# The head of a GRU kernel: the order of its weight loads, of its bias products and of the first turn of x

## The chip, the cores and the metric

The kernel runs on one core of a Trainium2 chip. The core has a matrix engine (TensorE, PE in the profile), a vector engine (VectorE, DVE), an activation engine (ScalarE, ACT), a general engine (GpSimd, POOL) and a queue engine (SyncE, SP). Transfers between DRAM and the core's memory are issued by SP, ACT or POOL and carried by 16 DMA engines. The metric is the device time of one execution in microseconds (us), the median of three runs.

## The reference, cut to what matters

A GRU runs over 256 time steps, and its states go through an expert-choice layer; x is added to the result.

```
x: [16, 256, 512]   W_ih, W_hh: [512, 1536]   b_ih, b_hh: [1536]   h0: [16, 512]
for t in 0..255:
    gi = x[:, t] @ W_ih + b_ih ;  gh = h @ W_hh + b_hh        # three gates of 512 columns: r, z, n
    r = sigmoid(gi_r + gh_r) ;  z = sigmoid(gi_z + gh_z)
    n = tanh(gi_n + r * gh_n)
    h = (1 - z) * n + z * h
y = expert-choice layer over the 4096 states (router softmax, top 256 tokens of each of 16 experts, one 512 x 512 matrix)
out = x + y
```

All of it is in float32. The steps are a chain: step t+1 can't start before h of step t is there.

## The kernel before, in words

The program has three stages: a head, a loop over the 256 steps, and a tail. The change touches the head only (lines 68 to 88, 440 to 474 and 722 to 777).

**Tiling.** Time is cut into 32 groups of 8 steps (TG = 8, NG = 32). A group of x is 128 rows (16 batch rows by 8 steps) of 512 columns, one slice `xs[:, g, :]`. W_ih lies in the tile `wih` in four row blocks k = 0..3, each 128 rows by 1536 columns (768 KB). W_hh lies in `whh`, and is loaded by gate: gate 0 is r, 1 is z, 2 is n, 1024 KB each. The input product of a pair p of steps, x times W_ih, is made by `x_part(p, k, bank, gates)` (line 613): four small matmuls for one row block k, each in its own quarter of the matrix engine. Its left operand is x turned, `xT`, which `spread_x` (line 729) makes: four transposes on TensorE into an idle PSUM bank, then four copies on VectorE, one for each pair of the group.

**Loads before (lines 453 to 474).** ACT's queue takes x's group 0, blocks 0 and 1 of W_ih, gate 0 and three quarters of gate 1 of W_hh. SP's queue takes blocks 2 and 3, x's group 1, gate 2, the last quarter of gate 1 and eight pieces of x's group 2 (`xa`, line 415). A one-element memset on POOL into block 2 (line 457) makes SP's first load wait a little. POOL's queue takes the initial state c0 and, at the end, the three bias rows (line 474).

**Work before (lines 722 to 777).** The order on PE, DVE, ACT and POOL is written out by hand. VectorE makes some masks (`make_masks`, from index rows that POOL writes); TensorE clears six PSUM banks (`begin_sums`, line 90, a bf16 matmul with zeros, 512 columns wide) and runs two more such matmuls to stay busy (`keep_clock`, line 717). Then `spread_x(0)`, two more idle matmuls, and the input product of the pairs 0 to 3 block by block, k = 0, 1, 2, 3. After block 1, c0 is turned (line 748). After block 2 come the bias products (`biases`, line 489: 16 matmuls of one or two rows that spread the biases over 128 rows into `l_bank`), two VectorE operations that copy them out (lines 756 and 757), and `spread_x(1)`. After block 3 come the sums `x_done` on VectorE, and the input products of the pairs 4 and 5, which need all four blocks, then one idle matmul, and step 0 begins (`h_part`, line 697, matmuls at line 705). `mixes` (line 640) are VectorE subtractions of blocks of W_ih for later products; part 0 needs blocks 0 and 1, part 1 needs all. Step 0 multiplies by the gates in the order r, n, r, n, z.

The loop and the tail are the same before and after.

Of the kernel before, what the change touches and what calls it, by code (L numbers as in the profile page):

```python
# [11 lines left out]
I32 = mybir.dt.int32  # L12
AF = mybir.ActivationFunctionType
ALU = mybir.AluOpType
# [3 lines left out]
def kernel(  # L18
# [27 lines left out]
    xs = const.tile([P, NG, D], F32, name="xs")  # L46
# [4 lines left out]
    wih = const.tile([P, KC, 3, D], F32, name="wih")  # L51
# [6 lines left out]
    GH = P // E  # L58
# [7 lines left out]
    ones_b = const.tile([P, B], F32, name="ones_b")  # L66
    zero = xs[:, NG - 1, D - P // 2 :].bitcast(BF16)
    nc.gpsimd.memset(zero, 0.0)
    make_identity(nc, ident)

    def make_masks():

        nc.gpsimd.memset(ones_b, 1.0)
        shift = GH.bit_length() - 1
        at = xs[:, 10, 0:3].bitcast(I32)
        nc.gpsimd.iota(at[:, 0:1], pattern=[[0, 1]], base=0, channel_multiplier=1)
        nc.vector.tensor_single_scalar(at[:, 1:2], at[:, 0:1], shift, ALU.logical_shift_right)
        nc.vector.tensor_single_scalar(at[:, 2:3], at[:, 0:1], GH - 1, ALU.bitwise_and)
        at_f = xs[:, 11, 0:3]
        nc.vector.tensor_copy(at_f, at)  # L80
        to_i = xs[:, 11, P : 3 * P].bitcast(I32).rearrange("p (o e h) -> p o e h", o=2, h=GH)
        nc.gpsimd.iota(to_i[:, 0, :, :], pattern=[[1, E], [0, GH]], base=0, channel_multiplier=0)
        nc.gpsimd.iota(to_i[:, 1, :, :], pattern=[[0, E], [1, GH]], base=0, channel_multiplier=0)
        to = xs[:, 10, P : 3 * P].rearrange("p (o n) -> p o n", o=2)
# [277 lines left out]
    with (  # L362
# [13 lines left out]
        bias = wts.tile([P, 4, P], F32, name="bias")  # L376
# [4 lines left out]
        C2 = 3 * P // 2  # L381
        spare = xs[:, RING:, :].rearrange("p g d -> p (g d)")[:, AHEAD * 3 * P : AHEAD * 3 * P + C2]
# [9 lines left out]
        c0 = xs[0:B, 7, :]  # L392
        ones = wts.tile([2, QD], F32, name="ones")
# [32 lines left out]
        def new_xa():  # L426
            return xap.tile([P, TG // 2, P], F32, name="xa")
# [12 lines left out]
        with tc.manual_schedule(engines={ET.SP, ET.Activation, ET.Pool}):  # L440
            def load_gate(gate, queue, ks=slice(0, KC)):
                queue.dma_start(
                    out=whh[:, ks, gate, :],
                    in_=w_hh[:, gate * D : (gate + 1) * D].rearrange("(c p) n -> p c n", c=KC)[:, ks, :],
                )

            def load_k(k, queue):
                queue.dma_start(
                    out=wih[:, k].rearrange("p g d -> p (g d)"),
                    in_=w_ih.rearrange("(p c) n -> p c n", c=KC)[:, k, :],  # L450
                )

            nc.scalar.dma_start(out=xs[:, 0, :], in_=x[:, 0:TG, :])
            load_k(0, nc.scalar)
            load_k(1, nc.scalar)
            nc.gpsimd.dma_start(out=c0, in_=cond)
            nc.gpsimd.memset(wih[0:1, 2, 0, 0:1], 0.0)
            load_k(2, nc.sync)
            load_k(3, nc.sync)
            nc.sync.dma_start(out=xs[:, 1, :], in_=x[:, TG : 2 * TG, :])  # L460
            load_gate(0, nc.scalar)
            load_gate(2, nc.sync)
            load_gate(1, nc.scalar, slice(0, KC - 1))
            load_gate(1, nc.sync, slice(KC - 1, KC))
            xa_next = new_xa()
            for c in range(KC):
                load_xa(2, xa_next, c, (nc.sync, nc.sync))
            nc.scalar.activation(dummy, ones[0:1, 0:1], AF.Sigmoid)
            for dst, src in (
                (b_raw[0:1], b_ih.rearrange("(o g d) -> o g d", o=1, d=D)),  # L470
                (b_raw[1:2], b_hh.rearrange("(o g d) -> o g d", o=1, d=D)),
                (b_n, b_hh[2 * D :].rearrange("(o d) -> o d", o=1)),
            ):
                nc.gpsimd.dma_start(out=dst, in_=src)

        def load_expert(part, s):

# [11 lines left out]
        def biases(bank):  # L489
            for i, rows in enumerate((b_raw[:, 0, :], b_raw[:, 1, :], b_raw[0:1, 2, :], b_n)):  # L490
                for j in range(KC):
                    nc.tensor.matmul(
                        bank[quadrant(j), P * i : P * (i + 1)],
                        ones[0 : rows.shape[0]],
                        columns(rows, j),
                        start=False,
                        stop=True,
                        tile_position=(0, QD * j),
                        skip_group_check=True,
                    )  # L500
# [216 lines left out]
        def keep_clock(n, banks=idles):  # L717

            for i in range(n):
                begin_sums(banks[i % len(banks)])  # L720

        with tc.manual_schedule(engines={ET.PE, ET.Activation, ET.DVE, ET.Pool}):
            make_masks()
            for bank in banks:
                begin_sums(bank)
            keep_clock(2)
            held = (r_bank, n_bank, z_bank, x_bank0, x_bank1, idles[1])

            def spread_x(g, bank):
                xT[g] = xtp.tile([P, TG // 2, P], F32, name="xt")  # L730
                for c in range(KC):
                    nc.tensor.transpose(bank[:, P * c : P * (c + 1)], xs[:, g, c::KC], ident)
                for q in range(TG // 2):
                    to = xT[g][:, q, :].rearrange("p (c o b) -> p c o b", c=KC, b=B)
                    nc.vector.tensor_copy(
                        to, bank.rearrange("p (c b t) -> p c t b", c=KC, t=TG)[:, :, 2 * q : 2 * q + 2, :]
                    )

            spread_x(0, idles[0])
            keep_clock(2, (idles[1],))  # L740
            for k in range(KC):
                for p in range(KC):
                    for gates in (slice(0, 1), slice(1, 3)) if p == k == 0 else (slice(0, 3),):
                        x_part(p, k, held[p], gates, start=False)
                if k == 1:
                    mixes(0)
                    for c in range(KC):
                        nc.tensor.transpose(
                            idles[0][:, B * c : B * (c + 1)], c0[:, P * c : P * (c + 1)], ident[0:B, 0:B]
                        )  # L750
                    nc.vector.tensor_copy(
                        hs[:, :, 0, :], idles[0][:, 0 : KC * B].rearrange("p (k b) -> p k b", b=B)
                    )
                elif k == 2:
                    biases(l_bank)
                    nc.vector.tensor_copy(bias, l_bank.rearrange("p (g d) -> p g d", d=P))
                    nc.vector.tensor_tensor(spare, bias_f[:, C2 : 2 * C2], bias_f[:, 0:C2], ALU.subtract)
                    spread_x(1, idles[0])
                    x_sums(1)
                elif k == 3:  # L760
                    mixes(1)
            for p in range(KC):
                x_done(p, held[p])
                if p == 0:
                    preset_first(0)
                elif p == 2:
                    preset_rest(0)
            for p in (KC, KC + 1):
                for k in range(KC):
                    for gates in (slice(0, 1), slice(1, 3)):  # L770
                        x_part(p, k, held[p], gates, start=False)
                if p == KC:
                    mixes(3)
                x_done(p, held[p])
# [6 lines left out]
        with tc.manual_schedule(engines={ET.PE, ET.Activation, ET.DVE, ET.Pool, ET.SP}):  # L781
# [6 lines left out]
            for s in range(T):  # L788
                p, odd = divmod(s, 2)
# [476 lines left out]
```

## Time and profile before

| what | us |
|---|---|
| median of three runs | 1114.39 (1114.12 to 1115.35) |
| the profiled execution, its own time | 1114.45 |
| its span in the trace | 1112.6 |
| first matmul of step 0 (line 705) | 25.72 |
| TensorE busy | 1101.7 (99% of the span) |

Times in the profile count from the start of the span. "PEld" is the weight load of TensorE, which runs beside its matmuls. A float32 matmul shows as two records. The end of a matmul is modelled, so that the distance from start to start is what a row of matmuls costs. A DMA's time "to landing" counts from the start of its issue until its semaphore says that all of it has arrived.

### The profile page before, as it was taken

The numbers are of one execution on the slowest core, as the hardware profiler recorded it, in microseconds if no ns is written. First come the engines' busy times: TensorE is split into PE (matmuls) and PEld (weight loads), VectorE is DVE, ScalarE is ACT, GpSimd is POOL, SyncE is SP. The second block draws the span as 40 slices with busy tenths as digits, with TensorE's granted clock in tenths as the row PEclk, the third lists the DMA queues.
The fourth block names the chain that finished last, engine by engine and source line by source line (L and its number), as shares of the span: only waits on it lengthen the run. The fifth ranks groups of instructions, "written<-read, shape, count | busy, mean of one in ns | idle before, by whom it ended". The sixth has DMA issues, their size and how long they took to land.

```text
span 1112.6 us, 77160 instructions
## 1 busy us (share of the span) xinstructions
PE 1101.7 (99%) x34291; PEld 957.8 (86%) x34291; DVE 802.0 (72%) x4664; ACT 579.0 (52%) x2644; POOL 30.0 (3%) x173
## 2 busy tenths in 40 slices
PE   9999999999999999999999999999999999999998
PEld 4888888888888888888888888888888888888763
DVE  4777666776777676767767677777777777777786
ACT  1555555555555555555555555555555555554551
POOL 1000000000000000000000000000000000000000
PEclk9999999999999999999999999999999999999999
DMA  7200000000000000000000000000000000002437
GB/s 258 63 11 12 12 12 14 19 21 21 21 21 12 12 14 14 14 14 12 12 12 12 14 14 14 14 12 12 12 12 14 14 15 14 4 4 80 136 108 238
DMA packets 34371, 37.34 MB, mean 34 GB/s; under 512 B 6112, under 2 KB 23776, under 8 KB 34032
## 3 DMA queue, kind: packets, MB, share of 16 engines
q1 hardware_dynamic: 32544, 28.64, 8.9%
q8 instruction: 270, 4.42, 1.6%
q10 hardware_dynamic: 1360, 3.67, 0.9%
q14 instruction: 69, 0.57, 0.2%
q0 software_dynamic: 128, 0.05, 0.0%
HBM read 23.94 MB, written 8.39 MB: 29 GB/s over the span
## 4 chain that ended last, share of the span: by engine, by line
PE 93%; DVE 4%; ACT 1%; DMA 1%; issue 0%; ACTq 0%; DVEq 0%
PE gates L705 59%; PE x L678 20%; PE gates L678 4%; PE pe L586 3%; PE x L308 3%; PE pe L308 2%; PE pe L115 1%; DVE nT L897 1%; DMA wih<-in_L_cond_W_ih_dram 1%; DVE t L859 1%; DVE zT L900 1%; PE gates L618 1%; ACT r L798 1%; ACT t L863 1%; PE x L618 0%
## 5 line engine op out<-in xcount | busy, mean ns | idle before, releaser
L705 PE MATMUL gates<-whh,hs 128*16 128x128 f32 x24576 | 722.1, 273 | 3.1 <-DVE hs L911 2.4
L705 PEld LDWEIGHTS gates<-whh,hs 128*16 128x16 f32 x24576 | 652.0, 103 | 57.0 <-DVE hs L911 50.5
L798 ACT ACTIVATE r<-gates 128x128 f32<-128x128 f32 x256 | 70.9, 277 | 232.8 <-PE gates L705 232.8
L802 DVE COPY seen<-r 1x1 f32<-1x1 f32 x256 | 36.3, 142 | 199.7 <-ACT r L798 199.4
L900 DVE STREAM_TRANSPOSE zT<-zs 128x32 f32<-128x32 f32 (+1 forms) x768 | 165.7, 216 | 0.0
L863 ACT ACTIVATE t<-t 128x64 f32<-128x64 f32 x512 | 103.1, 248 | 104.2 <-DVE t L861 104.2
L897 DVE STREAM_TRANSPOSE nT<-t 128x64 f32<-128x64 f32 x512 | 100.2, 234 | 48.1 <-ACT t L863 48.1
L908 DVE TENSOR_TENSOR v<-u,zT 128x32 f32<-128x32 f32 x512 | 98.7, 193 | 8.8
L911 DVE TENSOR_TENSOR hs<-v,nT 128x32 f32<-128x32 f32 x512 | 95.4, 186 | 8.7
L678 PE MATMUL x<-wih,xt 128*32 128x192 f32 (+2 forms) x1968 | 101.7, 325 | 0.0
L861 DVE TENSOR_TENSOR t<-t,xs 128x64 f32<-128x64 f32 x512 | 90.8, 220 | 0.0
L678 PE MATMUL x<-wih,xs 128*32 128x192 f32 x1952 | 90.5, 326 | 0.0
L859 DVE TENSOR_TENSOR t<-r,gates 128x64 f32<-128x64 f32 x512 | 90.3, 218 | 0.0
L865 ACT ACTIVATE zs<-gates 128x64 f32<-128x64 f32 x512 | 86.6, 221 | 0.0
L903 DVE TENSOR_TENSOR u<-hs,nT 128x32 f32<-128x32 f32 x512 | 78.3, 153 | 0.0
L678 PEld LDWEIGHTS x<-wih,xt 128*32 128x32 f32 x1968 | 62.4, 110 | 11.8
L678 PEld LDWEIGHTS x<-wih,xs 128*32 128x32 f32 x1952 | 62.2, 110 | 11.9
L511 ACT COPY ht<-hs 128x128 f32<-128x128 f32 (+1 forms) x128 | 52.0, 408 | 0.7 <-DVE hs L911 0.7
L678 PE MATMUL x<-xs 128*32 128x192 f32 (+1 forms) x1040 | 50.9, 316 | 0.0
L678 PE MATMUL x<-xs,xt 128*32 128x192 f32 x976 | 50.8, 326 | 0.0
L678 PE MATMUL gates<-xs 128*32 128x192 f32 x976 | 50.8, 326 | 0.0
L881 ACT COPY x<-x 128x192 f32<-128x192 f32 x61 | 18.5, 303 | 62.0 <-PE x L678 62.0
(199 smaller groups left out, 938.6 us busy)
## 6 DMA issues: line engine op xcount, KB each, us to landing
out_dram<-xs SPq DMA_DIRECT2D x31, 256.0 KB, 3.7
xa<-in_x_dram SPq DMA_DIRECT2D x240, 32.0 KB, 2.9
xs<-in_x_dram SPq DMA_DIRECT2D x27, 256.0 KB, 4.1
wih<-in_L_cond_W_ih_dram ACTq DMA_DIRECT2D x2, 768.0 KB, 6.4
wih<-in_L_cond_W_ih_dram SPq DMA_DIRECT2D x2, 768.0 KB, 9.6
whh<-in_L_cond_W_hh_dram ACTq DMA_DIRECT2D x1, 1024.0 KB, 15.7
whh<-in_L_cond_W_hh_dram SPq DMA_DIRECT2D x1, 1024.0 KB, 17.8
ewr<-in_L_ffn_expert_w_dram SPq DMA_DIRECT2D x4, 256.0 KB, 3.0
```

The lines of the kernel that those rows point to most:

```text
L678: nc.tensor.matmul(dst[quadrant(j), at:to], lhs[:, QD * k : QD * (k + 1)], columns(rows[k], j)[:, at // QD : to // QD], start=False, stop= ...
L705: nc.tensor.matmul(dst[quadrant(j, m)], lhs, columns(whh[:, k, gate_, :], j), start=False, stop=(k == KC - 1), tile_position=(0, QD * j), ...
L798: nc.scalar.activation(r, rr[p % 2], AF.Sigmoid)
L859: nc.vector.tensor_tensor(t[half], r[:, cols], hn[p % 2][:, cols], ALU.mult)
L861: nc.vector.tensor_tensor(t[half], t[half], ring[:, p % AHEAD, 2, cols], ALU.add)
L863: nc.scalar.activation(t[half], t[half], AF.Tanh)
L865: nc.scalar.activation(zs[half], zz[p % 2][:, cols], AF.Sigmoid)
L897: nc.vector.transpose(nT[half], t[half])
L900: nc.vector.transpose(zT[half][:, part], zs[half][:, part])
L903: nc.vector.tensor_tensor(u[half], hs[:, halves[half][2], slot(s), :], of_step(nT[half], odd), ALU.subtract)
L908: nc.vector.tensor_tensor(v[half], u[half], of_step(zT[half], odd), ALU.mult)
L911: nc.vector.tensor_tensor(hs[:, halves[half][2], slot(s + 1), :], v[half], of_step(nT[half], odd), ALU.add)
```

## The change

1. All four blocks of W_ih go on ACT's queue in order, behind x's group 0; block 0 goes in two transfers, r's columns (256 KB) and then z's and n's (512 KB). Gate 0 of W_hh follows on the same queue.
2. The three bias rows are the first loads of SP's queue; they were the last of POOL's.
3. The rest of SP's queue (x's group 1, gates 1 and 2 of W_hh, each in one transfer and in this order, then `xa`) is held until block 1 of W_ih has landed: POOL copies one element of block 1 into x's group 1.
4. The bias products come before `spread_x(0)` on TensorE; the two VectorE operations behind them and the masks come after `spread_x(0)`'s copies. The index rows of the masks are made by POOL during the loads (`number`).
5. In block 0 of the first product, r's columns of all four pairs come before z's and n's. For pair 4, the blocks 0 to 2 are taken three gates at once instead of r apart.

```diff
+    def number():
+        nc.gpsimd.iota(at[:, 0:1], pattern=[[0, 1]], base=0, channel_multiplier=1)
+        nc.gpsimd.iota(to_i[:, 0, :, :], pattern=[[1, E], [0, GH]], base=0, channel_multiplier=0)
+        nc.gpsimd.iota(to_i[:, 1, :, :], pattern=[[0, E], [1, GH]], base=0, channel_multiplier=0)
+        nc.gpsimd.memset(ones_b, 1.0)
+
     def make_masks():
-        nc.gpsimd.memset(ones_b, 1.0)
...
-        nc.gpsimd.iota(at[:, 0:1], pattern=[[0, 1]], base=0, channel_multiplier=1)
...
-        nc.gpsimd.iota(to_i[:, 0, :, :], pattern=[[1, E], [0, GH]], base=0, channel_multiplier=0)
-        nc.gpsimd.iota(to_i[:, 1, :, :], pattern=[[0, E], [1, GH]], base=0, channel_multiplier=0)
...
-            def load_k(k, queue):
+            def load_k(k, queue, gates=slice(0, 3)):
                 queue.dma_start(
-                    out=wih[:, k].rearrange("p g d -> p (g d)"),
-                    in_=w_ih.rearrange("(p c) n -> p c n", c=KC)[:, k, :],
+                    out=wih[:, k, gates].rearrange("p g d -> p (g d)"),
+                    in_=w_ih.rearrange("(p c) n -> p c n", c=KC)[:, k, gates.start * D : gates.stop * D],
                 )
-            nc.scalar.dma_start(out=xs[:, 0, :], in_=x[:, 0:TG, :])
-            load_k(0, nc.scalar)
-            load_k(1, nc.scalar)
-            nc.gpsimd.dma_start(out=c0, in_=cond)
-            nc.gpsimd.memset(wih[0:1, 2, 0, 0:1], 0.0)
-            load_k(2, nc.sync)
-            load_k(3, nc.sync)
-            nc.sync.dma_start(out=xs[:, 1, :], in_=x[:, TG : 2 * TG, :])
-            load_gate(0, nc.scalar)
-            load_gate(2, nc.sync)
-            load_gate(1, nc.scalar, slice(0, KC - 1))
-            load_gate(1, nc.sync, slice(KC - 1, KC))
-            xa_next = new_xa()
-            for c in range(KC):
-                load_xa(2, xa_next, c, (nc.sync, nc.sync))
-            nc.scalar.activation(dummy, ones[0:1, 0:1], AF.Sigmoid)
             for dst, src in (
                 (b_raw[0:1], b_ih.rearrange("(o g d) -> o g d", o=1, d=D)),
                 (b_raw[1:2], b_hh.rearrange("(o g d) -> o g d", o=1, d=D)),
                 (b_n, b_hh[2 * D :].rearrange("(o d) -> o d", o=1)),
             ):
-                nc.gpsimd.dma_start(out=dst, in_=src)
+                nc.sync.dma_start(out=dst, in_=src)
+            nc.scalar.dma_start(out=xs[:, 0, :], in_=x[:, 0:TG, :])
+            load_k(0, nc.scalar, slice(0, 1))
+            load_k(0, nc.scalar, slice(1, 3))
+            for k in range(1, KC):
+                load_k(k, nc.scalar)
+            load_gate(0, nc.scalar)
+            nc.gpsimd.dma_start(out=c0, in_=cond)
+            number()
+            nc.gpsimd.tensor_copy(xs[0:1, 1, 0:1], wih[0:1, 1, 0, 0:1])
+            nc.sync.dma_start(out=xs[:, 1, :], in_=x[:, TG : 2 * TG, :])
+            load_gate(1, nc.sync)
+            load_gate(2, nc.sync)
+            xa_next = new_xa()
+            for c in range(KC):
+                load_xa(2, xa_next, c, (nc.sync, nc.sync))
+            nc.scalar.activation(dummy, ones[0:1, 0:1], AF.Sigmoid)
...
-            make_masks()
             for bank in banks:
                 begin_sums(bank)
             keep_clock(2)
...
+            biases(l_bank)
             spread_x(0, idles[0])
+            make_masks()
             keep_clock(2, (idles[1],))
+            nc.vector.tensor_copy(bias, l_bank.rearrange("p (g d) -> p g d", d=P))
+            nc.vector.tensor_tensor(spare, bias_f[:, C2 : 2 * C2], bias_f[:, 0:C2], ALU.subtract)
             for k in range(KC):
-                for p in range(KC):
-                    for gates in (slice(0, 1), slice(1, 3)) if p == k == 0 else (slice(0, 3),):
+                for gates in (slice(0, 1), slice(1, 3)) if k == 0 else (slice(0, 3),):
+                    for p in range(KC):
                         x_part(p, k, held[p], gates, start=False)
...
                 elif k == 2:
-                    biases(l_bank)
-                    nc.vector.tensor_copy(bias, l_bank.rearrange("p (g d) -> p g d", d=P))
-                    nc.vector.tensor_tensor(spare, bias_f[:, C2 : 2 * C2], bias_f[:, 0:C2], ALU.subtract)
                     spread_x(1, idles[0])
                     x_sums(1)
...
             for p in (KC, KC + 1):
                 for k in range(KC):
-                    for gates in (slice(0, 1), slice(1, 3)):
+                    for gates in (slice(0, 1), slice(1, 3)) if p > KC or k == KC - 1 else (slice(0, 3),):
                         x_part(p, k, held[p], gates, start=False)
```

More of the change, by code (lines that the diff above doesn't have):

```diff
@@ L69 @@
     make_identity(nc, ident)
+    shift = GH.bit_length() - 1
+    at = xs[:, 10, 0:3].bitcast(I32)
+    at_f = xs[:, 11, 0:3]
+    to_i = xs[:, 11, P : 3 * P].bitcast(I32).rearrange("p (o e h) -> p o e h", o=2, h=GH)
+    to = xs[:, 10, P : 3 * P].rearrange("p (o n) -> p o n", o=2)
+    def number():
[3 more added lines that the diff above has]
+        nc.gpsimd.memset(ones_b, 1.0)
     def make_masks():
-        nc.gpsimd.memset(ones_b, 1.0)
-        shift = GH.bit_length() - 1
-        at = xs[:, 10, 0:3].bitcast(I32)
-        nc.gpsimd.iota(at[:, 0:1], pattern=[[0, 1]], base=0, channel_multiplier=1)
         nc.vector.tensor_single_scalar(at[:, 1:2], at[:, 0:1], shift, ALU.logical_shift_right)
         nc.vector.tensor_single_scalar(at[:, 2:3], at[:, 0:1], GH - 1, ALU.bitwise_and)
-        at_f = xs[:, 11, 0:3]
         nc.vector.tensor_copy(at_f, at)
-        to_i = xs[:, 11, P : 3 * P].bitcast(I32).rearrange("p (o e h) -> p o e h", o=2, h=GH)
-        nc.gpsimd.iota(to_i[:, 0, :, :], pattern=[[1, E], [0, GH]], base=0, channel_multiplier=0)
-        nc.gpsimd.iota(to_i[:, 1, :, :], pattern=[[0, E], [1, GH]], base=0, channel_multiplier=0)
-        to = xs[:, 10, P : 3 * P].rearrange("p (o n) -> p o n", o=2)
         nc.vector.tensor_copy(to, to_i.rearrange("p o e h -> p o (e h)"))
```

## The prediction, made before the changed kernel ran

> **What bounds the kernel now.** I read the page first: its row of TensorE says that almost the whole span is matmul, and the loop is the same in both kernels. So the head can only move the start of step 0, and all that follows shifts with it, microsecond for microsecond.
>
> ```profile
> PE 1101.7 (99%) x34291; PEld 957.8 (86%) x34291; DVE 802.0 (72%) x4664; ACT 579.0 (52%) x2644; POOL 30.0 (3%) x173
> ```
>
> Second, the chain of work that ended last, asked for the first 50 us (start, length, what). It is led by a transfer up to 10.01 and by TensorE alone from there to step 0 (line 705).
>
> ```profile
> 1.44 0.60 ACTq L448
> ...
> 2.07 7.90 DMA wih<-in_L_cond_W_ih_dram
> ...
> 10.01 2.14 PE gates L618 x24
> 12.16 0.65 PE x L618 x8
> 12.80 0.35 PE idle L748 x4
> 13.15 2.07 PE gates L618 x24
> 15.22 0.65 PE x L618 x8
> 15.86 1.01 PE gates L492 x32
> 16.87 0.68 PE idle L732 x4
> 17.55 2.07 PE gates L618 x24
> 19.62 3.25 PE x L618 x72
> 22.87 2.60 PE idle L618 x64
> 25.47 0.32 PE idle L93
> 25.79 1.48 PE gates L705 x48
> ```
>
> The reader should see two things that the change can take out: what lies before 10.01 (block 1 of W_ih is late), and the bias products (line 492), 1.01 us in the middle of TensorE's path. A row block of pairs 0 to 3 costs 2.07 + 0.65 = 2.72 us.
>
> Third, the timeline before 10.01, for the order on TensorE and VectorE (start, length):
>
> ```profile
> 3.53 1.06 PE L93 MATMUL idle<-xs 128*128 128x512 bf16 x2
> 4.45 1.10 PE L732 MATMUL idle<-ident,xs 128*128 128x128 f32 x4
> 5.34 1.06 PE L93 MATMUL idle<-xs 128*128 128x512 bf16 x2
> 5.58 0.88 DVE L735 COPY xt<-idle 128x128 f32<-128x128 f32 x4
> 6.44 2.21 PE L618 MATMUL gates<-wih,xt 128*32 128x128 f32 x32
> ```
>
> TensorE is in a row of work from 1.0 on, gets to the turn of x at 4.45, to block 0 at 6.44, and is through with it at 9.29 (8.46 + 0.83, its last records). Then it sits idle for 0.72 us until block 1 lands. The same 512-column idle matmul has 0.634 us early in the head and 0.389 us at 25.40; the early ones start 0.43 apart. So TensorE runs slower, up to half, before about 6.4. The granted clock is listed as 1.00 throughout, so the lengths have to tell it.
>
> Fourth, the transfers issued in the first 45 us (size, time from issue to landing):
>
> ```profile
> xs<-in_x_dram ACTq DMA_DIRECT2D x1, 256.0 KB, 3.6
> xs<-in_L_cond_b_ih_dram POOLq DMA_DIRECT2D x1, 6.0 KB, 5.7
> xs<-in_L_cond_b_hh_dram POOLq DMA_DIRECT2D x1, 2.0 KB, 6.5
> xa<-in_x_dram SPq DMA_DIRECT2D x10, 32.0 KB, 2.3
> ```
>
> x's group 0, issued at 0.75, lands at 4.35; that is what the turn of x waits for. The small pieces of xa on SP's queue land in 2.3 us, the bias rows on POOL's queue in 5.7 to 6.5.
>
> **The change part by part.**
>
> *Block 1 earlier.* From 4 to 6 us ACT's queue alone moves 0.76 MB, 0.38 per us; by 6.0 it has moved 1.22 MB. Before, SP's blocks 2 and 3 share the engines from about 6 on (both queues then show some 0.2 MB per us) and block 1 lands at 9.97. After, ACT's queue has x, block 0 and block 1 in front, 1.84 MB; the 0.62 MB left at 6.0 take 1.6 us. Block 0's data (1.05 MB by the same count) was through at 5.55 and landed at 6.34, so 0.8 us are added: block 1 lands at 8.4. Block 0's r columns come sooner than all of it, some 5.1; z's and n's stay near 6.4, and r's products of four pairs (0.9 us, a third of 2.72) cover them. The gap of 0.72 us goes if TensorE starts block 0 no later than before; what decides is when it starts.
>
> *Bias products before the turn of x.* 32 records, 1.01 us in the row at 15.86. They leave the middle, 1.01 us gained, and come back at the front. There they stand behind the first idle matmuls, which end at 4.39 (start 3.53 and two times 0.43). Their data: SP is free at 0.7 (its wait for the start ends there), three issues of about 0.4 us (the rows of xa have 0.31 to 0.43) put the last one at some 1.6; with 2.3 us it lands at 3.9, with the 6.5 of POOL's row at 8.1. I take 3.9, as it is the same queue; and all but the last quarter of the products need only the first two loads. So they start at 4.39, and at a slower matmul. The bounds: 1.01 us as at 15.86, and 2.0 us at half speed. The transposes give 1.3 between early and late (4.45 to 5.34 against 0.68), the 512-column rows at least 1.6 by length (0.634 to 0.389) and two if 0.43 is set against half of it. I take 1.8 us, since these products stream columns as the idle ones do: done at 6.2.
>
> *The turn of x.* Behind them the four transposes take 0.89 us as they did: 7.1. VectorE's first copy began 0.24 us after the transposes' end (5.34 to 5.58) and one of four takes 0.22. Before, the masks stood ahead of those copies on VectorE until 5.58; now they are behind, which gains nothing, since the transposes end later than that. The first product of block 0 can start at 7.1 + 0.24 + 0.22 = 7.56; the two idle matmuls beside it, by the row of 0.32 at 25.47, end no later than 7.75. I take 7.55. Pair by pair, one copy of 0.22 us feeds r's products of one pair, also some 0.22.
>
> *The sum.* Block 0 ends, and block 1 begins, at 7.55 + 2.72 = 10.27, against 10.01: 0.26 us lost. Block 1 has then long landed (8.4). From there the path is the old one less 1.01 us: step 0 starts 0.75 us earlier. The profiled execution of before was 1114.45 (span 1112.6 and 1.85 around it), the median 0.06 less: 1113.64, so 1113.6.
>
> *What costs nothing, and under which cover.* Pair 4 in three-gate products: pair 4 in 64 records (2.60, the rest of the 3.25) and pair 5 in 64 (2.60) cost what four parts of a block in 40 records cost (2.72 for four), so fewer records gain nothing; the r-first order of block 0 adds records at the same price. VectorE: the copies end at 8.2, masks 1.57 (4.01 to 5.58), the bias copy and difference 1.05, `mixes(0)` 1.76: 12.6. Its next work is c0's copy, for which TensorE's transposes come at 13.0; then TensorE has 2.72 us of block 2 before `spread_x(1)` needs that bank. Without that cover the surplus would be added one to one. POOL: it loses three issues (about 0.5 us each), makes three index rows and a memset (some 0.8 us), then waits for block 1; behind the waiting copy POOL has nothing until step 1. ACT: seven issues of about 0.55 us, then a table load of 1.28, all over by about 7; its first work is at 22.07.
>
> *The held queue.* Behind POOL's copy stand, on SP, x's group 1, gates 1 and 2 and xa. Block 1 at 8.4, the copy (0.17), an issue: first packets at about 10 (x's group 0 had 1.4 us from issue to first packet). Meanwhile ACT's queue goes on with block 2 (through at 9.7) and block 3, so the engines have no hole. Block 3 and x's group 1 share them and land at about 13.3; they are needed at 7.55 + 3 × 2.72 + 0.35 + 0.68 = 16.7 and 15.9. From 9.7 some 4.2 MB are left, at the 0.37 MB per us that both queues show from 16 to 19: 21.0, landing 22 to 23. Before, the last piece of W_hh was issued at 6.3 and landed 16.8 later, 23.1. Gate 2, now the last one, is needed 0.3 us into step 0 at about 25. Cover: some 2 us; each us beyond is lost one to one.
>
> **The rivals.**
>
> *A, above:* bias products on a slow TensorE; 0.75 us gained, by the unknown bounds 0.5 to 1.2.
>
> *B, TensorE at full speed early.* Nothing in the trace says what makes it fast at about 6.4; in a run where it comes at 4.4 the sum is 4.39 + 1.01 + 0.68 + 0.46 = 6.54 for block 0, 9.26 for block 1, 1.76 us gained: 1112.6. Against it: in the one trace, the row of 0.43 lasts to 6.2. Beyond it there is little: with no bias products at all before block 0, block 1 starts at 8.4 at the earliest (its landing), 2.6 us gained.
>
> *C, the other side: the bias rows are late and TensorE is idle in front.* They now stand ahead of the turn of x, and nothing can pass them. If b_n lands at time t, only the last quarter of the products (0.25 to 0.45), the transposes and a copy are behind it: block 1 at t + 4.3, a gain as long as t is below 6.7. With POOL's 6.5 us, t is 8.1 and the kernel 1.4 us slower: 1115.8. If the idle time also keeps TensorE slow through block 0 (up to 2.72 us more), the kernel is over 0.2% slower from t = 6.3 on, and at 8.1 it is 4.1 slower: 1118.5. For it: the bias rows took that long on POOL's queue, while block 0 was in flight. Against: SP issues them before ACT has issued W_ih at all.
>
> *D, gate 2 late:* landing at 26 takes the gain away, at 28 it costs 2.3: 1116.7. Against: the bytes are the same and the last ones have 2 us.
>
> [...]
>
> **How the numbers follow.** A 0.45, B 0.23, C 0.17 (half of it with slow matmuls), D 0.07; that something in the loop or the tail answers to the shift, either way by more than 2 us, 0.08. Some 0.2% (2.2 us) is what a measurement of this kernel can tell from no change. A, most of B, the mild half of C and half of D are within it: 0.66. Faster by more: the end of B and part of the rest, 0.18. Slower by more: the hard half of C, half of D and part of the rest, 0.16. The range leaves out the hard half of C and of D above and the rest below: 1112.0 to 1116.0.
>
> **What would show it.** In the changed profile: block 1 no longer a releaser of TensorE; line 492 starting at about 4.4 and taking 1.8 us (A), 1.0 (B), or waiting for a DMA (C); line 618 starting at 7.5; no gap from there to line 705, first at 25.0; gate 2 landing before 23.5. Wrong would make it above all a wait ahead of line 492, or a line 705 that waits for W_hh.

## The result, and the profile after

The changed kernel is slower by a little: 1116.41 us (median of 22 runs, 1115.83 to 1118.12) against 1114.78 for the kernel before (22 runs, 1114.08 to 1116.81), a ratio of 1.0014 with a 95% interval from 1.0008 to 1.0021. That is 1.6 us, 0.14%, where 0.8 us less was forecast; the range ended at 1116.0. The profiled execution took 1115.83, the shortest of the 22, with a span of 1114.0 (before 1114.45 and 1112.6); so the profile shows 1.4 of the 1.6 us.

The row of TensorE on the page answers to that of before: as many records, and busy for 0.9 us less, though the kernel takes longer.

```profile
PE 1100.8 (99%) x34291; PEld 957.2 (86%) x34291; DVE 801.7 (72%) x4664; ACT 579.5 (52%) x2644; POOL 29.0 (3%) x170
```

So the difference is idle time of TensorE. Step 0 (line 709 now) has its first matmul at 26.92 instead of 25.72, 1.20 us later, and the reset gate of a step near the end stands at 1019.03 instead of 1017.83, again 1.20 later. So all of the shift of the loop is made in the head. The chain of work that ended last, in the head of the changed kernel (start, length, what):

```profile
2.61 7.43 DMA wih<-in_L_cond_W_ih_dram
10.05 0.05 issue
10.10 0.18 POOL xs L471
...
10.30 7.61 DMA xs<-in_x_dram
17.91 0.14 issue
18.05 0.72 PE idle L735 x4
...
26.99 1.48 PE gates L709 x48
```

Before, TensorE led this chain from 10.01 on. Now two transfers lead it up to 17.91, joined by the held queue: block 1 of W_ih lands at 10.05, POOL copies its element, SP issues x's group 1 at 10.30, and that takes 7.61 us to land. The timeline of TensorE shows what the waits cost (start, length, what, and in brackets the idle time ahead with what ended it):

```profile
4.23 1.08 PE L496 MATMUL gates<-xs,ones 2*32 2x128 f32 x32
5.24 0.75 PE L735 MATMUL idle<-ident,xs 128*128 128x128 f32 x4
...
6.37 0.86 PE L622 MATMUL gates<-wih,xt 128*32 128x128 f32 x24
...
8.22 1.50 PE L622 MATMUL gates<-wih,xt 128*32 128x256 f32 x24 [0.76 <-DMA wih<-in_L_cond_W_ih_dram]
...
10.09 2.14 PE L622 MATMUL gates<-wih,xt 128*32 128x384 f32 x24
...
18.05 0.72 PE L735 MATMUL idle<-ident,xs 128*128 128x128 f32 x4 [2.11 <-DMA xs<-in_x_dram]
```

TensorE is through the bias products, the turn of x and block 0's r columns early, and then waits 0.76 us for block 0's z and n. Block 1 starts at 10.09 instead of 10.01, which is 0.08 us lost. The bias products no longer stand in the middle: 1.01 gained. Ahead of the second turn of x there is a wait that the kernel before didn't have, 2.11 us. The sum is 0.08 − 1.01 + 2.11 = 1.18, of the 1.20 found at step 0. The span is 1.4 longer; the last VectorE operation of the tail is still 1.21 late (1108.43 against 1107.22), so the other 0.2 come behind it.

That x's group 1 had to queue shows in the DMA queues (packets, MB, share of 16 engines; q10 is ACT's queue, q1 is SP's). From 13 to 14 us there is only ACT's:

```profile
q10 hardware_dynamic: 193, 0.40, 102.0%
```

and from 14 to 15 SP's has begun, with its first packet at 14.25, 4.0 us after the issue:

```profile
q10 hardware_dynamic: 119, 0.24, 66.9%
q1 hardware_dynamic: 66, 0.14, 41.5%
```

Last, the windows from 4 to 7 us (start and end, length, busy time and instructions of PE, PEld, DVE, ACT and POOL, granted clock, busy share of the DMA engines, GB/s):

```profile
4.00:5.00 1.00, 1.00 (x30) 0.77 (x32) 0.00 (x0) 0.00 (x0) 0.00 (x0) 1.00 1.01 279
5.00:6.00 1.00, 1.00 (x17) 0.71 (x10) 0.00 (x0) 0.00 (x0) 0.00 (x0) 1.00 0.98 262
6.00:7.00 1.00, 1.00 (x26) 0.57 (x28) 0.97 (x6) 0.00 (x0) 0.00 (x0) 1.00 0.78 240
```

And the same three windows in the kernel before:

```profile
4.00:5.00 1.00, 1.00 (x5) 0.58 (x4) 0.91 (x5) 0.99 (x1) 0.53 (x2) 1.00 0.97 375
5.00:6.00 1.00, 1.00 (x5) 0.43 (x3) 0.96 (x6) 0.20 (x1) 0.00 (x0) 1.00 0.99 393
6.00:7.00 1.00, 0.96 (x17) 0.51 (x20) 0.47 (x3) 0.00 (x0) 0.00 (x0) 1.00 1.05 429
```

The engines are as busy as then from 4 to 6, and move a quarter to a third less. Block 1, forecast to land at 8.4, came at 10.05; how much of that goes with the lower rate, the second experiment shows.

### The profile page after: what moved, and what is told of

Same layout as the page of the kernel before. It is cut to its first block, busy times and chain, and to the rows that moved or that the text cites. A ratio compares the mean times of both kernels' runs of the same rounds, so it can differ in the third digit from the quotient of the medians.

```text
span 1114.0 us, 77159 instructions
## 1 busy us (share of the span) xinstructions
PE 1100.8 (99%) x34291; PEld 957.2 (86%) x34291; DVE 801.7 (72%) x4664; ACT 579.5 (52%) x2644; POOL 29.0 (3%) x170
## 4 chain that ended last, share of the span: by engine, by line
PE 92%; DVE 4%; ACT 1%; DMA 1%; issue 0%; ACTq 0%; POOL 0%; DVEq 0%
PE gates L709 59%; PE x L682 20%; PE gates L682 4%; PE pe L590 3%; PE x L312 3%; PE pe L312 2%; PE pe L119 1%; DVE nT L901 1%; DMA xs<-in_x_dram 1%; DMA wih<-in_L_cond_W_ih_dram 1%; DVE t L863 1%; DVE zT L904 1%; ACT r L802 1%; ACT t L867 1%; DVE v L912 0%
## 6 DMA issues: line engine op xcount, KB each, us to landing
whh<-in_L_cond_W_hh_dram ACTq DMA_DIRECT2D x1, 1024.0 KB, 10.5
```

## The experiments

Two causes are to be told apart: the late x's group 1 (a queue held too long, then starved), and the slow data at the front (block 0 in pieces, or SP's small loads ahead of it, or something else). Ratios are against runs of the kernel before on the same chip in the same session: 1114.65, 1114.2, 1114.85 and 1114.64 in the four sessions. "Step 0" is the first matmul of step 0 on the timeline of the profiled execution, 25.72 before and 26.92 after (in a chain of work it stands 0.07 later).

### First session: one part of the change undone at a time

x's group 1 on ACT's queue, between blocks 1 and 2; only the gates and `xa` are held, until block 1 has landed.

```diff
-            for k in range(1, KC):
-                load_k(k, nc.scalar)
+            load_k(1, nc.scalar)
+            nc.scalar.dma_start(out=xs[:, 1, :], in_=x[:, TG : 2 * TG, :])
+            load_k(2, nc.scalar)
+            load_k(3, nc.scalar)
...
-            nc.gpsimd.tensor_copy(xs[0:1, 1, 0:1], wih[0:1, 1, 0, 0:1])
-            nc.sync.dma_start(out=xs[:, 1, :], in_=x[:, TG : 2 * TG, :])
+            nc.gpsimd.tensor_copy(whh[0:1, 0, 1, 0:1], wih[0:1, 1, 0, 0:1])
```

> Theory S (starved hold): x's group 1, issued on SP's queue at 10.30, gets its first packets only at about 14, behind what ACT's queue has lined up, and the 2.1 us for which TensorE waits for it are the whole loss. With group 1 on ACT's own queue between blocks 1 and 2 it lands by about 13, TensorE doesn't wait for it, and step 0 begins 2.1 us sooner than in the changed kernel, at 24.8 instead of 26.92; time about 1114.3, 0.5 under the kernel before. Rival H (W_hh is late anyway): gates 1 and 2, still held, land after 25, and step 0 waits for them: less than 1 us is won back.

Measured: 1116.54, ratio 1.0015 [1.0006, 1.0024], step 0 at 27.08. The wait for x is gone, and nothing came of it. The timeline of TensorE in this run has new waits at the blocks:

```profile
8.43 1.50 PE L623 MATMUL gates<-wih,xt 128*32 128x256 f32 x24 [0.85 <-DMA wih<-in_L_cond_W_ih_dram]
...
11.43 2.14 PE L623 MATMUL gates<-wih,xt 128*32 128x384 f32 x24 [1.07 <-DMA wih<-in_L_cond_W_ih_dram]
...
15.45 2.14 PE L623 MATMUL gates<-wih,xt 128*32 128x384 f32 x24 [0.89 <-DMA wih<-in_L_cond_W_ih_dram]
```

So the late x was one of two shortages; the other is slow data (336 GB/s at most from 4 to 11 us). Block 2, behind x's group 1, is late, and so is block 1, which stands ahead of it in the queue: TensorE starts on it at 11.43 instead of 10.09. In the trace a transfer's semaphore counts up in 16 steps; of block 1's, 15 are done by 10.11, and the last comes at 11.38. Why, no run shows. The gates of W_hh were not waited for here either.

Block 0 in one transfer, all else as after:

```diff
-            load_k(0, nc.scalar, slice(0, 1))
-            load_k(0, nc.scalar, slice(1, 3))
+            load_k(0, nc.scalar)
```

> Theory P (pieces): that block 0 goes in pieces of 2 and 4 KB rows is why the engines moved only 0.26 MB per us from 4 to 7 us, and why z's and n's columns landed at 8.1 and block 1 at 10.05 instead of 6.3 and 8.4. With block 0 whole, block 0 lands at about 6.5, block 1 at 8.6 to 9.0, TensorE's gap of 0.76 us goes, and x's group 1 is issued 1 us sooner; it is still starved, so step 0 comes 0.5 to 1.5 us sooner than in the changed kernel. Rival (the pieces are innocent, something else in the head slows the transfers): block 1 lands at 10 again, no change in time.

Measured: 1114.75, ratio 1.0002 [0.9993, 1.0011], step 0 at 25.57. The chain of work that ended last:

```profile
2.13 6.18 DMA wih<-in_L_cond_W_ih_dram
8.31 0.05 issue
...
8.66 7.91 DMA xs<-in_x_dram
16.56 0.14 issue
16.70 0.72 PE idle L734 x4
```

Block 1 lands at 8.31, where the prediction had it, and the windows from 4 to 7 show 362, 406 and 424 GB/s, as in the kernel before. The two pieces of block 0 are thus what made the data slow: this edit changes nothing else. From 2 to 8 us 0.45 MB more are moved than in the changed kernel; at the 0.41 MB per us of these windows that is about 1.1 of the 1.74 us by which block 1 lands sooner. The pieces also end raggedly: the 16 steps of the semaphore of z's and n's columns come from 5.9 to 8.2 in the changed kernel, those of the whole block 0 from 5.9 to 6.4 here. x's group 1 is still 7.91 us on its way and TensorE waits 1.29 us for it.

The bias products back behind block 2 (the two VectorE operations with them):

```diff
-            biases(l_bank)
             spread_x(0, idles[0])
...
                 elif k == 2:
+                    biases(l_bank)
+                    nc.vector.tensor_copy(bias, l_bank.rearrange("p (g d) -> p g d", d=P))
+                    nc.vector.tensor_tensor(spare, bias_f[:, C2 : 2 * C2], bias_f[:, 0:C2], ALU.subtract)
                     spread_x(1, idles[0])
```

> The changed kernel with the bias products and their copies back behind block 2, loads unchanged. Theory S: they (1.01 us) fit into the 2.1 us for which TensorE waits for x's group 1, so step 0 stays at 26.9 and the time within 0.3 us of the changed kernel. Rival: the products in front did gain 1.0 us and the loss is elsewhere: 1.0 us slower than the changed kernel.

Measured: 1116.32, ratio 1.0014 [1.0005, 1.0024], step 0 at 26.89, the same as after. The chain of work that ended last shows why:

```profile
16.10 1.08 PE gates L496 x32
17.21 0.70 DVE bias L760
18.02 0.72 PE idle L735 x4
...
26.96 1.48 PE gates L709 x48
```

The second turn of x begins at 18.02 (18.05 after). The chain names the bias copy, which ends at 17.91, but the semaphore of x's group 1 is full only at 17.89. With x landing there, the microsecond in front of it is free, wherever the bias products are. Their move was worth nothing in the changed kernel.

No hold: SP's queue starts at once, POOL only writes an element of x's group 1.

```diff
-            nc.gpsimd.tensor_copy(xs[0:1, 1, 0:1], wih[0:1, 1, 0, 0:1])
+            nc.gpsimd.memset(xs[0:1, 1, 0:1], 0.0)
```

> The changed kernel, but POOL writes a constant into x's group 1 instead of a copy of block 1's element, so that SP's queue goes on at about 2. Theory S: group 1 then lands well before 15.9, TensorE doesn't wait for it (2.1 us won), but SP's gates share the engines with blocks 1 to 3 and these come later: block 1 1 to 2 us later than 10.05, TensorE waits there. Together 0 to 1 us faster than the changed kernel. Rival (the hold itself is no matter, group 1 comes at 17.9 in any case): no change.

Measured: 1115.64, ratio 1.0009 [1.0000, 1.0018], step 0 at 26.07. No wait for x; TensorE waits 0.61 us for block 0 and 1.10 for block 1, which lands at 11.35, with SP's queue now sharing the engines from 7.5 on. The hold does what it says for block 1 (1.3 us), and costs more than that at x's group 1.

### Second session: parts done alone, and the two faults mended together

The bias part alone, on the kernel before: bias rows first on SP's queue, bias products ahead of the turn of x, the two VectorE operations behind its copies.

```diff
+            for dst, src in (
+                (b_raw[0:1], b_ih.rearrange("(o g d) -> o g d", o=1, d=D)),
...
+                nc.sync.dma_start(out=dst, in_=src)
             nc.scalar.dma_start(out=xs[:, 0, :], in_=x[:, 0:TG, :])
...
+            biases(l_bank)
             spread_x(0, idles[0])
             keep_clock(2, (idles[1],))
+            nc.vector.tensor_copy(bias, l_bank.rearrange("p (g d) -> p g d", d=P))
...
                 elif k == 2:
-                    biases(l_bank)
```

> The kernel before with one part of the change: bias rows first on SP's queue, bias products ahead of the turn of x, their copies behind it. Theory S/P (the bias part gains, the loads lose): TensorE reaches block 0 at about 7.0 and is through it by 9.7, block 1 lands at 10 as before, nothing else waits, and step 0 begins 1.0 us sooner than before, at 24.7: time 1.0 us under before. Rival (the gain of the bias part is not real, something later takes it back): same time as before within 0.3 us.

Measured: 1114.52 (1113.19 to 1116.48), ratio 0.9998 [0.9989, 1.0008]. No gain is shown. Its profiled execution was among the longer ones (1115.63, step 0 at 27.16). In it block 0 landed at 8.32 instead of 6.3, though the data moved about as fast as before (340, 387 and 449 GB/s from 4 to 7): 15 of the 16 steps of its semaphore are done by 6.24, the last comes at 8.32. Why is open. TensorE was idle for 1.74 us, and the granted clock went down, as the windows show:

```profile
6.00:8.00 2.00, 0.72 (x5) 0.21 (x3) 1.64 (x6) 0.21 (x2) 0.00 (x0) 0.99 1.04 433
8.00:10.00 2.00, 1.54 (x20) 1.12 (x24) 0.20 (x1) 0.00 (x0) 0.00 (x0) 0.50 0.99 406
```

The split alone, on the kernel before:

```diff
-            load_k(0, nc.scalar)
+            load_k(0, nc.scalar, slice(0, 1))
+            load_k(0, nc.scalar, slice(1, 3))
```

> The kernel before with block 0 of W_ih in two transfers, r's columns apart. Theory P: the transfers of 4 to 7 us move under 0.3 MB per us instead of 0.38 to 0.43, block 0 is complete at about 8 instead of 6.3, block 1 lands 1 to 2 us later than 9.97, and step 0 begins 1 to 2 us later than 25.72. Rival (the split does harm only with the order of the changed kernel): block 1 within 0.3 us of before.

Measured: 1119.1 (6 runs), ratio 1.0042 [1.0030, 1.0054]: 4.9 us slower from this edit, all of it in the head (step 0 at 30.80). The chain of work that ended last:

```profile
2.07 7.75 DMA wih<-in_L_cond_W_ih_dram
9.82 0.04 issue
9.86 3.64 PE gates L619 x24
```

Block 0 is complete at 9.82, against 6.3 in the kernel before; from 4 to 6 the engines move 248 and 257 GB/s. TensorE is idle for 3.50 us and then runs at a granted clock of 0.50 (windows of the same run):

```profile
8.00:10.00 2.00, 0.14 (x4) 0.14 (x8) 0.00 (x0) 0.00 (x0) 0.00 (x0) 0.71 1.03 400
10.00:12.00 2.00, 2.00 (x18) 0.66 (x18) 0.00 (x0) 0.00 (x0) 0.00 (x0) 0.50 0.99 397
```

In the changed kernel TensorE's idle time at that place is 0.76 us and its granted clock stays at 1.00: the bias products and r of all pairs cover most of the lateness.

Both faults mended: block 0 whole, and SP held only until block 0 has landed (edit against after).

```diff
-            load_k(0, nc.scalar, slice(0, 1))
-            load_k(0, nc.scalar, slice(1, 3))
+            load_k(0, nc.scalar)
...
-            nc.gpsimd.tensor_copy(xs[0:1, 1, 0:1], wih[0:1, 1, 0, 0:1])
+            nc.gpsimd.tensor_copy(xs[0:1, 1, 0:1], wih[0:1, 0, 0, 0:1])
```

> The changed kernel with block 0 whole and SP's queue held for block 0 instead of block 1. Theory S+P: x's group 1 is issued at about 6.6 and gets packets some 3.7 us later, from 10.3 on, lands at about 14.5, before TensorE asks for it at 15.3; block 1 lands at 8.3 as in the run with the whole block. TensorE then has no wait from block 0 to step 0, which begins at 24.3: 1.4 us under the kernel before, 1113.3. Rival: SP's gates share the engines with blocks 2 and 3, these land after 12.3 and 15.8, and TensorE waits for them instead: no gain over the run with the whole block.

Measured: 1114.46 (1112.54 to 1116.77), ratio 1.0001 [0.9990, 1.0012]; its profiled execution took 1112.62, with step 0 at 23.99. In that execution no wait is left in the head: on the timeline of TensorE all that the kernel has to do stands in one row.

```profile
4.36 1.08 PE L495 MATMUL gates<-xs,ones 2*32 2x128 f32 x32
...
15.11 0.72 PE L734 MATMUL idle<-ident,xs 128*128 128x128 f32 x4
...
23.99 2.82 PE L708 MATMUL gates<-whh,hs 128*16 128x128 f32 x96
```

This is 1.73 us ahead of the kernel before, the prediction's rival B nearly to the digit (1.76), though B was worked out for other loads. But the twelve times lie in two groups, six from 1112.54 to 1113.53 and six from 1115.39 to 1116.77, and the median gains nothing.

The same with the bias products back behind block 2 (the edit of the third run):

> The same with the bias products and their copies back behind block 2. Theory: with no wait left to swallow them they cost their 1.0 us of TensorE, less what TensorE's earlier start of block 0 meets at block 1's landing (8.3): 0.3 to 1.0 us slower than the kernel with the products in front. Rival (the bias part is worth nothing in any order): same time.

Measured: 1113.85 (1112.96 to 1116.28), ratio 0.9998 [0.9989, 1.0006], step 0 at 24.84. Nine of the twelve times are below 1114.2. The profiled head is 0.85 longer than with the bias products in front; the median is not, since fewer of its times are long.

### Third session: the two groups of times, and the split under other conditions

The kernel with both faults mended, unchanged, for two more profiled executions:

> The kernel with the whole block 0 and SP's queue held for block 0 once more, for a second profile: its times spread from 1112.5 to 1116.8, and the profile taken showed 1112.6. Theory C (TensorE idle in front, then slow): where it takes 1115 or more, TensorE waits for the bias rows or for block 0, and its matmuls of block 0 then take up to twice as long, some 3 us in all before step 0. Rival: the head is the same and the spread lies in the loop or the tail.

> As the run before it, a third profile, so that one of the upper times is likely among them; the same expectations.

One came out at 1112.75 (step 0 at 23.79), the other at 1115.12 (26.60). The chain of work of the first:

```profile
4.35 1.01 PE gates L495 x32
5.36 0.68 PE idle L734 x4
6.03 0.43 PE idle L97 x2
6.47 0.84 PE gates L621 x24
```

and of the second, the same four groups:

```profile
4.60 1.86 PE gates L495 x32
6.46 1.06 PE idle L734 x4
7.52 0.85 PE idle L97 x2
8.37 1.44 PE gates L621 x24
```

The same 32 bias products take 1.01 or 1.86 us, the turn of x 0.68 or 1.06, r of block 0 0.84 or 1.44. No transfer is waited for in either, so the expected wait is not the cause. TensorE is at full speed from before 4.4 in the one and only from about 10 in the other, and that makes all of the 2.8 us between them. That this is what parts the two groups of times rests on this one slow profile of the kernel.

The changed kernel with SP held until block 0's r columns have landed, and block 0 still in two pieces:

```diff
-            nc.gpsimd.tensor_copy(xs[0:1, 1, 0:1], wih[0:1, 1, 0, 0:1])
+            nc.gpsimd.tensor_copy(xs[0:1, 1, 0:1], wih[0:1, 0, 0, 0:1])
```

> The changed kernel with SP's queue held for block 0's r columns instead of block 1, block 0 still in two pieces. Theory S+P: x's group 1 is issued at about 6 and lands before 15, so the wait of 2.1 us for it goes, but block 1, already late at 10.05 through the pieces, now shares the engines and comes at 10.5 to 11.4 as without the hold: step 0 at about 25.3 to 26.1, 0.8 to 1.6 us faster than the changed kernel, 1114.8 to 1115.6. If only the hold were to blame, it would do as well as with the whole block (step 0 at 23.9).

Measured: 1114.99 (1114.03 to 1117.57), ratio 1.0003 [0.9994, 1.0012]. By the medians (1.0014 for after) the earlier hold alone takes back most of the loss, though the two intervals overlap. Eight of the eleven times are below the shortest of after, though the two weren't measured side by side. The profiled execution had the slow TensorE (bias products 1.86, step 0 at 26.33), which hides the late block 0, so it doesn't show what the split costs here.

Block 0 in two transfers of 64 rows, on the kernel before: two transfers, but each row still 6 KB long.

```diff
-            load_k(0, nc.scalar)
+            for ps in (slice(0, P // 2), slice(P // 2, P)):
+                nc.scalar.dma_start(
+                    out=wih[ps, 0].rearrange("p g d -> p (g d)"),
+                    in_=w_ih.rearrange("(p c) n -> p c n", c=KC)[ps, 0, :],
+                )
```

> The kernel before with block 0 of W_ih in two transfers as well, but by rows: 64 rows of the whole 6 KB each. Theory P (short pieces of rows are slow, not the second transfer): the engines keep 0.38 MB per us from 4 to 6 us, block 0 is complete by about 6.5, time within 0.5 us of before. Rival (any second transfer delays what follows): as the split by columns, 4 to 5 us slower than before.

Measured: 1119.42 (5 runs), ratio 1.0042 [1.0028, 1.0055], as bad as the split by columns. Block 0 is complete at 9.61; from 4 to 7 us the windows show 217, 214 and 227 GB/s, with the engines 97 to 99% busy. So short rows are not needed for the loss; the theory that they alone are the cause falls. It doesn't clear them either: two half-height transfers may be slow for a reason of their own.

### Fourth session: what sets TensorE's speed, and a split elsewhere

By now the open question was whether the bias products, which use one or two rows of the matrix engine, keep it slow. The mended kernel with the bias products behind the transposes of x, in place of two idle matmuls:

```diff
-            biases(l_bank)
             spread_x(0, idles[0])
+            biases(l_bank)
             make_masks()
-            keep_clock(2, (idles[1],))
```

> The kernel with the whole block 0 and SP's queue held for block 0, with the bias products behind the transposes of x's group 0, in the place of the two idle matmuls, so that they run while VectorE copies and block 0 (6.4) is on its way. Theory C: block 0 no longer waits for the products in runs in which TensorE is slow until late; step 0 at 23.8 in a fast head and 25 in a slow one, median about 1113.3, and fewer times above 1115 than with the products in front (6 of 12). Rival: the upper times have nothing to do with where the products stand: as many of them.

Measured: 1115.43 (1113.36 to 1118.22), ratio 1.0005 [0.9995, 1.0015]; the profiled execution, the shortest of the twelve, has step 0 at 23.88.

And with one 512-column idle matmul behind every fourth bias product:

```diff
-        def biases(bank):
+        def biases(bank, idle=lambda: None):
...
+                idle()
...
-            biases(l_bank)
+            biases(l_bank, lambda: keep_clock(1, (idles[1],)))
```

> The same kernel with the products in front as in the change, and one 512-column idle matmul behind every fourth of them (four in all). Theory C: the products of one or two rows are not enough work to bring the clock up; with the idle matmuls among them the clock comes up by 7 us in every run, the times of 1115 and more go, median about 1113.3 (0.2 us for each idle matmul at full speed). Rival (when the clock comes up is chance, whatever TensorE does between 4 and 7 us): the times spread from 1112.5 to 1116.8 as before.

Measured: 1117.35 (1114.05 to 1118.71), ratio 1.0015 [1.0003, 1.0026]; step 0 at 25.23 in the profiled execution, again the shortest. Long times didn't become rarer in either: six of twelve are above 1115.4 in the one, eight of twelve above 1115.8 in the other. That the bias products in front keep TensorE slow is not shown. These two runs give it no support, but they don't rule it out: neither has a profile of a long execution, and the kernel before, too, has 6 of its 27 times beside them above 1116, so that the long times need not come from the head.

Block 1 in two transfers by columns, on the kernel before:

```diff
-            load_k(1, nc.scalar)
+            load_k(1, nc.scalar, slice(0, 1))
+            load_k(1, nc.scalar, slice(1, 3))
```

> The kernel before with block 1 in two transfers by columns instead of block 0. Theory P (pieces of 2 and 4 KB rows move slowly): blocks 0 lands at 6.3 as before, block 1 1 us or more later than 9.97, TensorE waits longer and loses its clock: 1 to 4 us slower than before. Rival (the pieces only do harm at the very start, behind x's group 0 and beside the first transfers of the other queues): within 0.5 us of before.

Measured: 1118.65 (9 runs), ratio 1.0027 [1.0018, 1.0037]. In the head it costs 0.87 us (timeline of TensorE):

```profile
10.87 2.14 PE L619 MATMUL gates<-wih,xt 128*32 128x384 f32 x24 [1.68 <-DMA wih<-in_L_cond_W_ih_dram]
...
26.59 2.81 PE L706 MATMUL gates<-whh,hs 128*16 128x128 f32 x96
```

Block 1 lands at 10.74 instead of 9.97. The data rate stays where it was (393, 361 and 446 GB/s from 4 to 7), so a split is not slow everywhere. The rest of this execution's 4.8 us arises late in the loop: five steps from 1018.94 to 1042.92 take 24.0 us instead of 20.3, with TensorE idle for nothing that the profile shows. Why is open. In all the other traces it is 1086.7 to 1087.7 us from step 0 to the end of the span, in this one 1090.8.

No version is shown to beat the kernel before: the best median is 0.35 us below it, within its interval.

## Why the prediction was wrong

**The step that failed is *The held queue*.** It let x's group 1 have its first packets at about 10 and land at 13.3, 2.6 us ahead of need. The need was right: TensorE came to the second turn of x at 15.94 (18.05 − 2.11), against 15.9 in the text, whose own terms add to 16.06. The landing was 17.91. Of these 4.6 us, 1.65 are block 1's lateness, which the hold passes on. Then, 4.0 us instead of 1.4 went by from the issue to the first packets, and the transfer took 3.7 us from there instead of 3.3; the last 0.9 of these are the wait for the last of its semaphore's 16 steps (15 are done by 16.97). The 1.4 had been read off x's group 0, which was issued on empty engines. The trace of before had a better row: SP's block 2, issued at 2.40 behind ACT's backlog, has its first packet between 5.5 and 6. And the same price recurs: with block 0 whole, x's group 1 is issued at 8.66 and has its first packets after 12.5; with the hold on block 0 it is issued at 6.78, begins after 10.5 and lands at 14.98; without the hold it is issued at 3.06 and begins after 7.5. From issue to landing it is 7.6, 7.9 and 8.2 us in the three that are held. Releasing SP at block 1 was thus late by construction; the text took the hold for a matter of who shares the engines, and the run without it shows that this was worth 1.3 us at block 1.

**Block 1 earlier** was right for a block 0 in one transfer: 8.31 measured with it, 8.4 forecast. For the changed kernel it was wrong by 1.65 us, because the step counted only bytes at the old rate. It split block 0 at no cost; the runs show the rate a quarter to a third lower from 4 to 6 us, z's and n's columns landing at 8.2 instead of near 6.4, and, on the kernel before, 4.9 us for the split alone. No bound for the price of a split stood in the prediction: its two transfers were nowhere in the trace of before, and the step should have bounded them from both sides as it did with the bias products.

**Bias products before the turn of x**: the start was right (4.23, forecast 4.39), and the bias rows were there in time, so that C did not happen. Both prices named for them exist: 1.01 us in the profiled execution of after, which is case B, and 1.86 in two others, which is case A's 1.8. Which of them comes differs from one execution of the same kernel to the next.

**The turn of x** began block 0 at 6.37, as B has it (6.54) and not A (7.55). **The sum** then failed only by the wait: without it, step 0 would have stood at 26.92 − 2.11 = 24.81, 0.91 earlier than before, beside the 0.75 of the forecast. That nearness is in part luck: block 0 began 1.2 us earlier than forecast, and the wait of 0.76 us for z's and n's columns, which the forecast had covered, took much of it back. The mended kernel's 23.99 is B's gain.

**What costs nothing** held: the row with pair 4 takes 3.23 us in 48 records, 3.25 in 72 before; the VectorE work and POOL's index rows are on no chain of after. ACT's issues are, up to 2.61, and up to 2.07 in the kernel before: the second piece of block 0 puts the issue of block 1 0.54 us later. ACT is through with its loads and its table at 9.9 instead of 7, still long before its first work at 22.92. **D** didn't happen; no matmul of step 0 waits for W_hh. (Its price for a landing at 28 should be 2.0 by the text's own 0.3 us into step 0, not 2.3.)

The other side came about by a mechanism that none of the rivals named: x's group 1, the first transfer behind the hold. The text had even asked who waits behind POOL's copy, and answered it with a margin of 2.6 us worked out from the wrong row. That the loss of 0.14% is within the 0.2% that had the largest chance is no merit of the working.

In the kernel before, with both queues at work, ACT's shows 158 packets and SP's 156 from 12 to 14 us, 0.32 MB of each. In the changed kernel 4.0 us pass before SP's queue shows the first packet of x's group 1. Where in between issue and engine the delay lies, no run here shows.

## What to carry to other kernels

Here a transfer that waited for another transfer's landing paid the full way from issue to landing (7.6 to 8.2 us behind a backlog, against 3.6 for x's group 0 on empty engines); take that price from a transfer issued onto busy engines, not from the first of the program. A split of a load is an edit of its own, to be tried alone: here it cost 4.9 us alone on the kernel before, more than all else in the change could bring (1.73 in the profile of the mended kernel). And when an early part of a chain is made shorter, look for the next item that is released by an event instead of by the engine itself, since it may take the gain.

## What had not been expected of the hardware

- **A load in two transfers.** Two transfers in place of one for block 0 cut the rate from 375 to 430 GB/s down to about 250 (by columns) or 220 (by rows), with the DMA engines busy for 74 to 99% of the time from 4 to 6 us. For block 1, whose two transfers were issued 0.5 to 0.6 us later on the same queue, the rate stayed (393, 361 and 446 GB/s). The cause is open.
- **TensorE's speed in the head.** The same kernel on the same chip has its early matmuls at full speed from before 4.4 us or only from about 10 (the 32 bias products take 1.01 or 1.86 us), a difference of 2.8 us at the end, though TensorE is in a row of work from 1.0 in both and the granted clock is listed as 1.00 in both. What decides it is open; it blurs any change of the head that is smaller.
- **A short idle time can cost the clock.** In the run with 1.74 us of idle time the granted clock was 0.50 from 8 to 10 us, and block 0's 32 records in `gates` took 3.57 us instead of the 2.21 of the kernel before. In the run with 3.50 us it was 0.50 to 0.58 from 10 to 16 us. The waits of the changed kernel, 0.76 and 2.11, and the 1.68 of the last run left it at 1.00. By the windows, the granted clock is 0.99 from 6 to 8 us and 0.50 from 8.0 in the run with 1.74, some 1.3 us after TensorE's last work, and 0.93 from 8 to 9 and 0.50 from 9.0 in the run with 3.50, some 2.6 us after it. The 2.11 of the changed kernel shows that a gap longer than that 1.3 need not cost it. What tells these cases apart, no run shows.
